# Reordering the second product of a fused attention kernel and shifting its operands by 64 bytes

One core of one Trainium2 chip. The metric is the device time of one execution in microseconds (us), the slowest core's, as the median of several runs. All runs quoted were at full TensorE clock (granted 0.998 or 0.999) unless a line says more.

## The reference

Attention over the 4,096 positions of four images, 128 channels for q and k, 256 for v, then a residual sum (biases and all but the layer's core left out):

```
q = x Wq + bq;  k = x Wk + bk;  v = x Wv + bv          # x: (4, 64, 64, 256)
energy    = einsum('bcn,bcm->bnm', pq, pk)             # pq, pk: (4, 128, 4096)
attention = softmax(energy, axis=-1)
out       = einsum('bcm,bnm->bcn', pv, attention)      # pv: (4, 256, 4096)
return gamma * out.reshape(x.shape) + x
```

## The kernel before

The kernel works on 16 groups of 256 columns n per image, and in each on eight steps t of 512 rows m. It gets float32 accuracy out of TensorE's float32r by splitting operands: p = exp(energy) goes to h (rounded down), l and d (combinations of the rest), v to vh, vl and vd. A step has three parts on TensorE: twelve matmuls of energies for a step three ahead (weights k, moving rows q), and the second product of its own step, 24 matmuls: h with vh, l with vl, d with vd, for two blocks j of n and four blocks i of m. In each, a slice of h, l or d is the weights, and a row of v (258 or 256 numbers per partition) moves.

```python
xpool, xtpool, qkv = pool("xpool", 3), pool("xtpool", 3), pool("qkv", 1)
ppool, work, kpool = pool("ppool", 2), pool("work", 2), pool("kpool", 3)
...
vh = qkv.tile([P, NM, VC], F32R, tag="vh", name="vh")     # NM = 32 rows, VC = C + 4 = 260
vl = qkv.tile([P, NM, VC], F32R, tag="vl", name="vl")     # columns C, C+1 are ones: the sums
vd = qkv.tile([P, NM, C], F32R, tag="vd", name="vd")
...
def energy(b, u, k):
    ...
    for i in range(2):
        for to, f, first, last in ((sa, 0, True, False), (sa, 1, False, True), (sb, 2, True, True)):
            nc.tensor.matmul(
                to[:, i], kt[:, 2 * k + i, f, :], q[:, :, f, :], start=first, stop=last
            )
...
def attend(b, u, j):
    ...
    for out_, left, right in ((a, h, vh), (a, l, vl), (bb[:, j, :], d, vd)):
        for i in range(4):
            m = 2 * t + i // 2 + NI * (i % 2)
            nc.tensor.matmul(
                out_, left[:, i, n], right[:, m, : out_.shape[1]],
                start=..., stop=..., skip_group_check=True,
            )
...
for k in range(2):
    if ahead < STEPS:
        energy(b, ahead, k)
    ...
for j in range(NJ):
    attend(b, u, j)
```

Tiles lie one behind another in SBUF in the order in which their pools are made: x's, then vh, vl, vd, then ppool (x, y, h, l, d), work (q among others), kpool (k).

## Time and profile before

| | before |
|---|---|
| time, median (range) of the runs beside the changed kernel | 2500.35 us (2498.88 to 2501.34) |
| PE busy / weight loads busy | 99% / 98% |
| VectorE / ScalarE busy | 84% / 72% |

How to read what follows: matmuls overlap in the trace and their ends are modelled, so I use **start-to-start times**: from one matmul's start to the next one's. Their sum is the time of TensorE's stream. In a timeline line, the first number is the start of the first of the merged instructions, so the difference of two lines' starts divided by the count is the mean start-to-start time. The lines of before that matter are shown in the prediction.

### The profile page before, as it was taken

What the parts mean: (1) busy time and instruction counts of PE and PEld (TensorE: products, weight loads), DVE (VectorE), ACT (ScalarE), POOL (GpSimd) and SP (SyncE); (2) the same over time, 40 slices, a digit from 0 to 9 for tenths busy, and PEclk for the clock granted to TensorE, in tenths of its full rate; (3) what the DMA queues carried; (4) which work ended last, traced back from release to release, by engine and by line L of the source; (5) the groups of instructions that cost most, each with busy time, mean ns of one, the idle gap of its engine ahead of it and who ended that gap; (6) DMA issues with size and microseconds to landing.
All of it is one profiled execution on the core that took longest, in us unless ns stands there. A gap on an engine that the chain in (4) does not pass through costs nothing.

```text
span 2497.3 us, 50025 instructions
## 1 busy us (share of the span) xinstructions
PE 2483.7 (99%) x19982; PEld 2442.8 (98%) x19982; DVE 2103.2 (84%) x2440; ACT 1807.1 (72%) x3138; POOL 425.7 (17%) x780
## 2 busy tenths in 40 slices
PE   9999999999999999999999999999999999999998
PEld 8999999999899999999989999999998999999998
DVE  5888888888698888888869888888886988888887
ACT  5777777776677777777667777777766777777775
POOL 4211111111411111111041111111114111111110
PEclk9999999999999999999999999999999999999999
DMA  7766666664766666666477666666648666666663
GB/s 240 219 193 208 202 207 195 193 209 148 242 214 196 202 202 208 200 194 204 138 245 220 202 190 207 206 202 197 192 144 255 212 203 198 196 208 203 200 194 106
DMA packets 137408, 498.92 MB, mean 200 GB/s; under 512 B 15536, under 2 KB 57264, under 8 KB 137168
## 3 DMA queue, kind: packets, MB, share of 16 engines
q0 software_dynamic: 92320, 453.17, 58.2%
q1 hardware_dynamic: 44304, 42.22, 5.6%
q8 instruction: 160, 2.62, 0.4%
q14 instruction: 80, 0.66, 0.1%
q10 hardware_dynamic: 544, 0.26, 0.0%
HBM read 445.25 MB, written 50.33 MB: 198 GB/s over the span
## 4 chain that ended last, share of the span: by engine, by line
PE 97%; ACT 2%; DVE 1%; issue 0%; DMA 0%; SPq 0%; ACTq 0%; DVEq 0%
PE a L364 38%; PE bb L364 19%; PE sa L316 19%; PE sb L316 10%; PE qk L136 4%; PE v L157 4%; PE ot L410 1%; PE xt L123 1%; ACT h L335 1%; DVE x L330 1%; ACT x L320 0%; ACT y L320 0%; DVE vd L283 0%; DMA x<-in_x_dram 0%; ACT vh L280 0%
## 5 line engine op out<-in xcount | busy, mean ns | idle before, releaser
L320 ACT ACTIVATE x<-sa 128x512 f32<-128x512 f32 x1024 | 608.8, 595 | 409.2 <-PE sa L316 329.6
L330 DVE TENSOR_TENSOR x<-x,y 128x1024 f32<-128x1024 f32 x512 | 625.8, 1222 | 159.2 <-ACT y L320 159.2
L316 PE MATMUL sa<-q,k 128*128 128x256 f32 x4096 | 749.9, 281 | 0.3
L364 PE MATMUL a<-vh,h 128*128 128x258 f32 x4096 | 661.2, 283 | 0.0
L364 PE MATMUL a<-vl,l 128*128 128x258 f32 x4096 | 658.2, 283 | 0.0
L364 PE MATMUL bb<-vd,d 128*128 128x256 f32 x4096 | 654.3, 282 | 0.0
L316 PEld LDWEIGHTS sa<-q,k 128*128 128x128 f32 x4096 | 625.7, 189 | 1.7 <-ACT x L320 1.1
L344 DVE SCALAR_TENSOR_TENSOR d<-h,x 128x1024 fp32r<-128x1024 f32 x512 | 624.2, 1219 | 0.0
L341 DVE TENSOR_TENSOR l<-x,h 128x1024 fp32r<-128x1024 f32 x512 | 624.1, 1219 | 0.0
L320 ACT ACTIVATE y<-sb 128x512 f32<-128x512 f32 x1024 | 612.8, 598 | 0.0
L316 PE MATMUL sb<-q,k 128*128 128x256 f32 x2048 | 578.6, 283 | 0.0
L335 ACT ACTIVATE h<-x 128x1024 fp32r<-128x1024 f32 x512 | 543.7, 1062 | 38.5 <-DVE x L330 37.7
L364 PEld LDWEIGHTS a<-vl,l 128*128 128x128 f32 x4096 | 563.6, 190 | 0.0
L364 PEld LDWEIGHTS bb<-vd,d 128*128 128x128 f32 x4096 | 560.6, 189 | 0.0
L364 PEld LDWEIGHTS a<-vh,h 128*128 128x128 f32 x4096 | 559.1, 189 | 0.0
L300 POOL DMA_DIRECT2D k<-kf x512 | 280.4, 548 | 1488.9 <-PE sb L316 1466.5
L316 PEld LDWEIGHTS sb<-q,k 128*128 128x128 f32 x2048 | 384.4, 188 | 8.1 <-ACT y L320 0.8
L136 PE MATMUL qk<-wqk_sb,xts 128*128 128x256 f32 x512 | 121.3, 380 | 0.0
L157 PE MATMUL v<-xts,wv_sb 128*128 128x256 f32 x512 | 120.3, 379 | 0.0
L157 PEld LDWEIGHTS v<-xts,wv_sb 128*128 128x128 f32 x512 | 97.3, 190 | 13.2
L402 ACT ACTIVATE o<-o,r 128x256 f32<-128x256 f32 x126 | 57.5, 504 | 72.5 <-DVE r L385 72.5
L136 PEld LDWEIGHTS qk<-wqk_sb,xts 128*128 128x128 f32 x512 | 92.3, 190 | 10.4 <-ACT xts L129 0.5
(54 smaller groups left out, 883.5 us busy)
## 6 DMA issues: line engine op xcount, KB each, us to landing
k<-kf POOLq DMA_DIRECT2D x512, 768.0 KB, 4.8
x<-in_x_dram SPq DMA_DIRECT2D x128, 256.0 KB, 3.7
kf<-f POOLq DMA_DIRECT2D x64, 384.0 KB, 4.0
out_dram<-x POOLq DMA_DIRECT2D x63, 256.0 KB, 2.5
qd<-qks POOLq DMA_DIRECT2D x128, 64.0 KB, 2.9
qr<-qd SPq DMA_DIRECT2D x64, 128.0 KB, 3.0
wv_sb<-in_L_conv_Wv_dram POOLq DMA_DIRECT2D x1, 256.0 KB, 5.7
out_dram<-x SPq DMA_DIRECT2D x1, 256.0 KB, 4.0
```

The lines of the kernel that those rows point to most:

```text
L123: nc.tensor.transpose(tp[:, k, s, :], self.xs[i][:, s, k * P : (k + 1) * P], ident,)
L136: nc.tensor.matmul(qk[:, s, :], self.xt[i][:, k, s, :], wqk_sb[:, k, :], start=(k == 0), stop=(k == KC - 1),)
L157: nc.tensor.matmul(vp[:, eh, :], wv_sb[:, k, eh * P : (eh + 1) * P], self.xt[i][:, k].rearrange("p s a -> p (s a)"), start=(k == 0), stop= ...
L300: nc.gpsimd.dma_start(t.rearrange("p (i s) f d -> p i s (f d)", s=2), kf[b, u % NU])
L316: nc.tensor.matmul(to[:, i], kt[:, 2 * k + i, f, :], q[:, :, f, :], start=first, stop=last)
L320: nc.scalar.activation(to[:, 2 * k : 2 * k + 2, :], sp.rearrange("p i j d -> p i (j d)"), AF.Exp, scale=scale,)
L330: nc.vector.tensor_tensor(x, x, y, ALU.mult)
L335: nc.scalar.activation(h, units[b, u], AF.Identity, scale=UPPER)
L341: nc.vector.tensor_tensor(l, x, h.bitcast(F32), ALU.subtract)
L344: nc.vector.scalar_tensor_tensor(d, h.bitcast(F32), 1.0 + E, x, ALU.mult, ALU.subtract)
L364: nc.tensor.matmul(out_, left[:, i, n], right[:, m, : out_.shape[1]], start=(t == i == 0 and (left is h or left is d and j == 0)), stop=(t ...
L402: nc.scalar.activation(o[:, j, :], o[:, j, :], AF.Identity, scale=r[:, j : j + 1])
```

## The change

Its intent: the same matmuls in another order and place. All of h's products, then all of l's, then all of d's, so that d's eight run into the twelve energies; and a pad of 64 bytes behind v, which shifts everything that follows. Cut to its core:

```diff
         xpool, xtpool, qkv = pool("xpool", 3), pool("xtpool", 3), pool("qkv", 1)
+        pool("pad", 1).tile([P, 16], F32, name="pad")
         ppool, work, kpool = pool("ppool", 2), pool("work", 2), pool("kpool", 3)
@@
-        def attend(b, u, j):
+        def attend(b, u):
@@
-            for out_, left, right in ((a, h, vh), (a, l, vl), (bb[:, j, :], d, vd)):
-                for i in range(4):
-                    m = 2 * t + i // 2 + NI * (i % 2)
-                    nc.tensor.matmul(out_, left[:, i, n], right[:, m, : out_.shape[1]], ...)
+            for left, right in ((h, vh), (l, vl), (d, vd)):
+                for j in range(NJ):
+                    out_ = bb[:, j, :] if left is d else acc[j]
+                    for i in range(4):
+                        m = 2 * t + i // 2 + NI * (i % 2)
+                        nc.tensor.matmul(out_, left[:, i, j * P : (j + 1) * P], right[:, m, : out_.shape[1]], ...)
@@
-                for j in range(NJ):
-                    attend(b, u, j)
+                attend(b, u)
```

More of the change, by code (lines that the diff above doesn't have):

```diff
@@ L347, in halves @@
             units[b, u] = h, l, d
-        def attend(b, u, j):
+        def attend(b, u):
             g, t = divmod(u, NU)
-            if t == j == 0:
+            if t == 0:
                 now["acc"] = [
@@ L357, in attend @@
             h, l, d = units[b, u]
-            a, bb = now["acc"][j], now["bb"]
-            n = slice(j * P, (j + 1) * P)
-            for out_, left, right in ((a, h, vh), (a, l, vl), (bb[:, j, :], d, vd)):
-                for i in range(4):
-                    m = 2 * t + i // 2 + NI * (i % 2)
-                    nc.tensor.matmul(
-                        out_,
-                        left[:, i, n],
-                        right[:, m, : out_.shape[1]],
-                        start=(t == i == 0 and (left is h or left is d and j == 0)),
-                        stop=(t == NU - 1 and i == 3 and left is not h),
-                        skip_group_check=True,
-                    )
-            if t == NU - 1 and j == NJ - 1 and (b, g) != (B - 1, NG - 1):
+            acc, bb = now["acc"], now["bb"]
+            for left, right in ((h, vh), (l, vl), (d, vd)):
[3 more added lines that the diff above has]
+                        m = 2 * t + i // 2 + NI * (i % 2)
+                        nc.tensor.matmul(
+                            out_,
+                            left[:, i, j * P : (j + 1) * P],
+                            right[:, m, : out_.shape[1]],
+                            start=(t == i == 0 and (left is h or left is d and j == 0)),
+                            stop=(t == NU - 1 and i == 3 and left is not h),
+                            skip_group_check=True,
+                        )
+            if t == NU - 1 and (b, g) != (B - 1, NG - 1):
                 now["o"] = work.tile([P, NJ, C], F32, tag="o", name=f"o_{b}_{g}")
```

## The prediction

> **What bounds the kernel now.** I read the page first: the busy table and the chain that ended last.
>
> ```profile
> PE 2483.7 (99%) x19982; PEld 2442.8 (98%) x19982; DVE 2103.2 (84%) x2440; ACT 1807.1 (72%) x3138; POOL 425.7 (17%) x780
> PEclk9999999999999999999999999999999999999999
> PE 97%; ACT 2%; DVE 1%; issue 0%; DMA 0%; SPq 0%; ACTq 0%; DVEq 0%
> PE a L364 38%; PE bb L364 19%; PE sa L316 19%; PE sb L316 10%; PE qk L136 4%; PE v L157 4%; PE ot L410 1%; PE xt L123 1%; ACT h L335 1%; DVE x L330 1%; ACT x L320 0%; ACT y L320 0%; DVE vd L283 0%; DMA x<-in_x_dram 0%; ACT vh L280 0%
> ```
>
> TensorE is the end of the kernel: 97% of the chain, at full clock, and its weight loads are busy for 98% of the span. 57% of the chain are the second product's matmuls (L364: a from h and l, bb from d), 29% the energies (L316). Nobody can take work from the path here; the only thing to win is the pace of one matmul after another. So next I read the waits of PE, and then its timeline.
>
> ```profile
> PE wp L197 <- POOL ident masks.py:199: 2.4, 1, 2.4
> PE ot L451 <- DVE o L446: 1.5, 1, 1.5
> PE xt L123 <- DMA x<-in_x_dram: 1.0, 1, 1.0
> ```
>
> The matmuls' own waits in the whole span are these 5 us. Now the timeline of PE in a quiet stretch (columns: start us, length us, engine, line, operation, operands, count). The lengths overlap and are modelled; the starts are what I use.
>
> ```profile
> 404.06 0.40 PE L316 MATMUL sa<-q,k 128*128 128x256 f32 x2
> ...
> 405.48 0.64 PE L364 MATMUL a<-vh,h 128*128 128x258 f32 x4
> 405.96 0.65 PE L364 MATMUL a<-vl,l 128*128 128x258 f32 x4
> 406.44 0.64 PE L364 MATMUL bb<-vd,d 128*128 128x256 f32 x4
> 406.92 0.64 PE L364 MATMUL a<-vh,h 128*128 128x258 f32 x4
> 407.40 0.65 PE L364 MATMUL a<-vl,l 128*128 128x258 f32 x4
> 407.88 0.64 PE L364 MATMUL bb<-vd,d 128*128 128x256 f32 x4
> 408.37 0.39 PE L316 MATMUL sa<-q,k 128*128 128x256 f32 x2
> ...
> 409.73 0.65 PE L364 MATMUL a<-vh,h 128*128 128x258 f32 x4
> ```
>
> The reader is to see two things. The twelve energies that start at 404.06 take until 405.48, 1.42 us or 118 ns each; the twelve that start at 408.37 take 1.36 us, 113 ns each. They are the same instructions on the same shapes with the same operands' spacing. And the second product takes 0.47 to 0.49 us for four, 118 to 122 ns each, whether its moving rows are 258 or 256 wide.
>
> I then took the start-to-start time of every matmul from the trace, leaving out those over 160 ns. Means: h 120.0 ns, l 120.0, d 119.1 (4096 of each), energies 116.2 (6144). I also sorted the energy blocks by their pace. Of 436 undisturbed blocks of twelve, 174 (40%) run at 113.3 ns throughout, but for at most the first, and 262 (60%) at 117.8 ns throughout. I call these **locked** and **unlocked**. No undisturbed unlocked block becomes locked midway. Which it will be is fixed by the step: with t the step of eight within a group, the energies after t = 4, 5 and 6 are nearly always locked, those after t = 1, 2, 3 and 7 unlocked (t = 0 has the output transposes in between). The pattern repeats from group to group to the nanosecond, so it comes from operands' addresses and timing and not from what other engines happen to do. Sorting d's matmuls by the ScalarE or VectorE operation beside them moves their mean by under 2 ns, with no sign that any one of these writes is the cause.
>
> **Where the change's 64 bytes come in.** From the code, per partition: d's tile lies 73,728 bytes behind vd's (vd itself 32,768, then ten tiles of 4,096), a multiple of 1,024, and rows and slices of both step in multiples of 512. So d's weights and the moving vd rows begin at the same place modulo 512: distance 0. k lies 16,448 bytes behind q, 64 over a multiple of 1,024, and steps in multiples of 512: distance 64. Distance 64 is the pair that can lock; distance 0 never stays at 113 ns in this trace. vh and vl have rows of 1,040 bytes, so their distance to h and l walks by 16 bytes from row to row and passes through every value.
>
> **What the Trainium skill says.** "TensorE: Matmul & The Clock Gate", LDWEIGHTS (loading the stationary operand): 128 columns take 128/1.2 = 107 ns. Back-to-back issue gap, same page: 256 moving columns at full clock take 256/2.4 + 2.5 = 109 ns. So loading and multiplying are balanced; the trace's best is 113.3 ns, a little above both, and the mean of the second product is 7 ns above that. The page "SBUF — State Buffer", Who interferes with whom, gives TensorE two independent read ports (moving rows and weights) and says that it never waits on anyone. The trace does not bear that out fully: two paces for the same energies. "Perfetto Trace Analysis", Identifying the Most-Contended Engine, tells to judge TensorE by the busy share of weight loads: 98%, which agrees with a path made of load, matmul, load. No page states a rule on the distance of weights and moving rows.
>
> **The change part by part.** It removes nothing and adds no instruction on TensorE: 12,288 matmuls of the second product before and after.
>
> 1. *The pad.* All tiles after v's shift by 64 bytes. q and k shift together, so the energies keep distance 64. d gets distance 64 from vd, exactly the energies'. h and l move by 64 against vh and vl. That is a step of four rows, two steps of t; since t runs through all values, the same set of distances occurs, only at other t. So I expect no change of the mean for h and l, 120.0 ns.
>
> 2. *The order.* Before, a step is E(12) h l d h l d with four of each; after, E(12) h(8) l(8) d(8). So each d block runs into the next energies, and the eight d's and twelve energies become one run of 20 with one distance. If the state is kept through a run, as it is in the energies now, all 20 are at 113.3 or all at 117.8 ns. The switch from one form to another has no cost of its own in the trace (h to l 120.8 ns beside 120.9 inside h), so having fewer switches saves nothing as such.
>
> 3. *How often a run locks.* The entry is now from l's last product. I can't read its phase out of a trace of before, so I take the share at which energies lock now on coming from another distance: 40%, or 3 of 7 values of t. Blocks that were broken by the transposes lock somewhat more often. I choose 45%. Pace: 0.45 x 113.3 + 0.55 x 117.8 = 115.8 ns.
>
> 4. *Sum.* d: (119.1 - 115.8) x 4,096 = 13.5 us saved. Energies: (116.2 - 115.8) x 6,144 = 2.5 us saved. Together 16 us. All of it is on TensorE, thus on the path. 2501 - 16 = 2485 us.
>
> 5. *Beside the path.* At a group's end the sums of a0 and a1 are now whole some 1 us earlier, but the kernel waits for bb's copy by ScalarE before VectorE frees a0 and a1; bb ends at the same place. In the group change that I looked at, a1 is free at 422.66 us. Its next use comes 4 matmuls after a0's at 422.50 instead of 12, at about 423.04: 0.4 us to spare. The first h of a group already loses 56 ns (a semaphore instruction of 51 ns in the weight queue): 63 x 56 ns = 3.5 us; a second one for a1 would cost 3 us, which I count in the range. l and d are needed later within a step than before, so VectorE (84% busy) gains slack.
>
> **The rivals.** (a) *All runs lock*, as the change's wording hopes: d and energies at 113.3, (119.1 - 113.3) x 4,096 + (116.2 - 113.3) x 6,144 = 24 + 18 = 42 us, 2459 us. For it: one distance throughout, and a locked block stays locked. Against it: 60% of the energy blocks don't lock today with that very distance, and the entry still comes from l, whose distance walks. (b) *None lock*: d 117.8 saves 5 us, the energies lose 1.6 x 6,144 = 10 us: 2506 us. For it: the new entry could miss at every t, since the outcome is fixed by t and not random; against it: eight values of t, of which 3 of 7 hit now. (c) *h and l move too*: runs of eight at one form could meet better or worse phases. Their times spread by some 3 ns over the steps' positions; over about 60 to 130 different positions the mean is good to 0.3 to 0.4 ns, that is 3 us of their 8,192. (d) *A wait takes the gain*: in the energies after the output transposes two or three intervals of about 200 ns wait for ScalarE to free their buffers; there a faster TensorE only waits longer. That is 60 of 512 blocks, some 10% of the energies' part.
>
> **Range and chances.** Step 3 is nearly all of the uncertainty. With eight values of t locking at 45%, the share has a spread of 0.18, times 4.5 ns x 10,240 = 8 us; with (c) and the semaphore some 10 us. The change was evidently made by someone who saw the energies' pace, so I lean a little to the faster side: 2483 us, range 2464 to 2498. Faster by over 2% needs under 2451 us, beyond even rival (a), and so h and l faster by over 1 ns each as well: 4%. Slower by over 2% (2551 us) has no mechanism but a new wait: 1%. Within 2%: 95%.
>
> **What would show it.** d's mean start-to-start time falls to 114 to 118 ns and takes the same two values as the energies; in the timeline a d block of eight (about 0.91 or 0.94 us) and the energies after it have one pace. h and l stay within 0.5 ns of 120.0. The share of locked energy blocks says where in the range the time falls. PE's waits stay at some 5 us, clock and counts unchanged. It is wrong if d and the energies after it don't share a pace, if d stays at 119 ns, if h or l move by over 1 ns, or if a wait for a1 or bb appears at the group changes.

## The result

2494.33 us (2493.11 to 2495.51, four runs) against 2500.35: ratio 0.9976, 95% interval 0.9959 to 0.9994. A ratio is the mean time of one kernel's fast runs over that of the other's of the same rounds, so not quite the ratio of the medians quoted. The time lies within my range, but the gain is 6 us where I had forecast 18.

The page of the changed kernel, busy times and chain:

```profile
PE 2478.3 (99%) x19982; PEld 2436.0 (98%) x19982; DVE 2108.0 (85%) x2440; ACT 1808.3 (73%) x3138; POOL 425.0 (17%) x780
PEclk9999999999999999999999999999999999999999
PE 97%; ACT 2%; DVE 1%; issue 0%; DMA 0%; SPq 0%; ACTq 0%; DVEq 0%
```

The bound is the same: TensorE, full clock, the same 19,982 matmuls. Its waits, from the waits of PE, have not grown either:

```profile
PE wp L197 <- POOL ident masks.py:199: 2.4, 1, 2.4
PE xt L123 <- DMA x<-in_x_dram: 1.2, 1, 1.2
PE ot L455 <- DVE o L450: 1.1, 1, 1.1
PE sa L318 <- ACT x L322: 0.7, 4, 0.2
```

So again everything is in the pace. Sums of start-to-start times in the two traces, in us, with the mean in ns of those from 100 to 160 ns, and, for the energies, the share of undisturbed blocks of twelve that I count as locked. Undisturbed means that no start-to-start time in the block is over 160 ns; locked, that the mean of its first eleven is under 115.5 ns:

| | before: sum, mean | after: sum, mean | difference |
|---|---|---|---|
| h (4,096) | 495.0, 120.0 | 493.2, 119.6 | -1.8 |
| l (4,096) | 491.5, 120.0 | 491.1, 119.9 | -0.4 |
| d (4,096) | 489.1, 119.0 | 478.4, 116.5 | -10.7 |
| energies (6,144) | 736.1, 116.1 | 743.3, 117.0 | +7.2 |
| all else | 274.7 | 275.0 | +0.4 |
| locked energy blocks | 174 of 432 (40%) | 64 of 432 (15%) | |

Two thirds of what d gained went back in the energies. The count of locked blocks hides a difference in kind: in before, 172 of the 174 are at 113 ns from the second matmul on; in the changed kernel none of the 64 is. They start at 118 ns, behind d's that were unlocked, and come down to 113 at the fifth matmul. The timeline of PE in the changed kernel shows how (start us, length us, engine, line, operation, operands, count):

```profile
411.22 1.07 PE L368 MATMUL bb<-vd,d 128*128 128x256 f32 x8
412.13 0.40 PE L318 MATMUL sa<-q,k 128*128 128x256 f32 x2
...
413.54 1.13 PE L368 MATMUL a<-vh,h 128*128 128x258 f32 x8
414.50 1.12 PE L368 MATMUL a<-vl,l 128*128 128x258 f32 x8
415.46 1.10 PE L368 MATMUL bb<-vd,d 128*128 128x256 f32 x8
```

The eight d's take 0.91 us, 113.8 ns each: they have locked. The twelve energies right behind them take 1.41 us, 117.5 ns each: they have not. In the trace, 243 undisturbed energy blocks follow a d that was locked (its fifth to seventh times under 115 ns), and not one of them is locked.

### The profile page after: what moved, and what is told of

It is laid out like the page before. It is cut to its first block, busy times and chain, and to the rows that moved or that the text cites. A ratio compares the mean times of both kernels' runs of the same rounds, so it can differ in the third digit from the quotient of the medians.

```text
span 2492.0 us, 50085 instructions
## 1 busy us (share of the span) xinstructions
PE 2478.3 (99%) x19982; PEld 2436.0 (98%) x19982; DVE 2108.0 (85%) x2440; ACT 1808.3 (73%) x3138; POOL 425.0 (17%) x780
## 4 chain that ended last, share of the span: by engine, by line
PE 97%; ACT 2%; DVE 1%; issue 0%; DMA 0%; SPq 0%; ACTq 0%; DVEq 0%
PE a L368 38%; PE sa L318 19%; PE bb L368 19%; PE sb L318 10%; PE qk L136 4%; PE v L157 4%; PE ot L414 1%; PE xt L123 1%; ACT h L337 1%; DVE x L332 1%; ACT x L322 0%; ACT y L322 0%; DMA x<-in_x_dram 0%; DVE vd L285 0%; ACT vh L282 0%
## 5 line engine op out<-in xcount | busy, mean ns | idle before, releaser
L368 PE MATMUL a<-vh,h 128*128 128x258 f32 x4096 | 576.6, 283 | 0.0
L368 PE MATMUL a<-vl,l 128*128 128x258 f32 x4096 | 574.2, 283 | 0.0
L368 PE MATMUL bb<-vd,d 128*128 128x256 f32 x4096 | 559.9, 279 | 0.0
L368 PEld LDWEIGHTS a<-vl,l 128*128 128x128 f32 x4096 | 526.9, 190 | 0.0
L368 PEld LDWEIGHTS a<-vh,h 128*128 128x128 f32 x4096 | 524.0, 189 | 0.0
L368 PEld LDWEIGHTS bb<-vd,d 128*128 128x128 f32 x4096 | 515.1, 189 | 0.0
L398 DVE SCALAR_TENSOR_TENSOR o<-a,o 128x256 f32<-128x256 f32 x126 | 47.5, 419 | 87.2 <-ACT o L378 87.2
```

The costliest lines, as they stand in the source:

```text
L368: nc.tensor.matmul(out_, left[:, i, j * P : (j + 1) * P], right[:, m, : out_.shape[1]], start=(t == i == 0 and (left is h or left is d and ...
L398: nc.vector.scalar_tensor_tensor(o[:, j, :], a[:, :C], 1.0 + E, o[:, j, :], ALU.mult, ALU.add)
```

## The experiments

First, what I had overlooked. I call *distance* the place of the weights that are loaded beside a matmul less the place of its moving rows, within a partition, modulo 512. Weights are loaded one matmul ahead (in before, the load for the h that starts at 401.21 us starts at 401.10, just behind the start of the last energy at 401.09), so at the boundary the pair is vd's row and **k**. The pad shifts k as well as d. So k, which had stood 64 behind vd's places, now stands 128 behind; and q, which had stood at vd's own places (modulo 512), stands 64 behind. The run of 20 "with one distance" that I had predicted has 64 seven times, 128 once, 64 again, and its moving rows change place in between.

My theory for the experiments: the distance of each pair sets the pace, a settled state is carried on only if nothing changes at the boundary. The rivals: the order itself brought d's gain; or the switch from d's to the energies' operands unlocks whatever the places.

Places modulo 512, behind vd's row, in the kernels compared, worked out from the tiles' sizes and order in the code (the traces hold no addresses):

| | order | h, l, d | q | k | d's pairs | boundary | energies' pairs |
|---|---|---|---|---|---|---|---|
| before | old | 0 | 0 | 64 | 0 | 64 | 64 |
| after | new | 64 | 64 | 128 | 64 | 128 | 64 |
| order alone | new | 0 | 0 | 64 | 0 | 64 | 64 |
| pad alone | old | 64 | 64 | 128 | 64 | 128 | 64 |
| one distance | new | 64 | 0 | 64 | 64 | 64 | 64 |
| two pads | new | 64 | 128 | 192 | 64 | 192 | 64 |

### The order alone

The changed kernel without the line `pool("pad", 1).tile([P, 16], F32, name="pad")`.

> The new order alone, without the pad: d's weights at distance 0 from vd's rows, k at 64 from both q and vd. Theory (the distance between a matmul's moving rows and the weights that are loaded beside it sets the pace; order alone is neutral): d stays at 118.5 to 119.5 ns, h and l at 120 within 0.6 ns, and 2493 to 2505 us, with the share of locked energy blocks the only thing that moves it. Rival 1 (the order itself, runs of eight of one form, brought d's gain): d at 116.8 ns as after, energies no worse, under 2492 us.

Measured: 2510.37 us (before on the same chip 2501.45, ratio 1.0035, 1.0021 to 1.0048): **slower than before** by 0.35%, and 5 us over my upper end. d 118.8 ns and h and l 120.4 and 119.9, as expected; but not one of 432 undisturbed energy blocks is locked, and the energies went to 117.9 ns. Rival 1 falls: the order alone gives d nothing. And the share of locked blocks, 40% before, isn't a property of the energies but of how each step enters them.

### The pad alone

```diff
+        pool("pad", 1).tile([P, 16], F32, name="pad")
         ppool, work, kpool = pool("ppool", 2), pool("work", 2), pool("kpool", 3)
```

> The pad alone, in the old order: d at 64 from vd, but k now at 128 from vd (64 from q). Theory: d's fours lock in part, d 116 to 118 ns; the last d before the energies loads k at distance 128, stalls (118 ns or more), and the energies are locked in under 25% of undisturbed blocks, mean 116.8 or more; 2492 to 2502 us. Rival 1 (order is what helps d): d at 119 ns, energies 40% locked as before, 2500 us.

Measured: 2498.94 us (ratio 0.9989, 0.9983 to 0.9996). d 117.7 ns and the last d 119.1 as expected. But 184 of 431 energy blocks (43%) are locked where I had expected under 25%, and the energies' mean is 116.2 ns, under my 116.8. None of the 184 is locked from its start: they begin at 117 to 118 ns and come down to 113 at the fifth or sixth matmul. So a stalled boundary doesn't keep energies from settling later; why some steps do and others don't is not shown.

### One distance

```diff
-        pool("pad", 1).tile([P, 16], F32, name="pad")
-        ppool, work, kpool = pool("ppool", 2), pool("work", 2), pool("kpool", 3)
+        work, kpool, ppool = pool("work", 2), pool("kpool", 3), pool("ppool", 2)
```

work and kpool together take 45,120 bytes, 64 over a multiple of 1,024, so h, l and d come to 64 behind v's places with no pad, while q and k stay where they were.

> The new order, no pad; the tiles of q and k are placed ahead of those of h, l and d. So q stands at 0, k at 64 and h, l, d at 64 from v's rows: every matmul from the first d to the last energy has one distance, the boundary from d to k too. Theory (the boundary at distance 128 cost the lock): d as after, 116 to 117 ns, the last d no slower than the others, and blocks that are locked at d's end stay so: at least 45% of undisturbed energy blocks locked, energies at 115.9 ns or less, 2478 to 2489 us, faster than both kernels. Rival 2 (the switch from d's to the energies' operands unlocks, whatever the distance): last d at 118 or more, energies under 25% locked, 2491 to 2498 us.

Measured: **2483.06 us** (2482.59 to 2484.97), ratio to before 0.9926, 0.9912 to 0.9939. Its interval lies wholly below the changed kernel's, so it beats both. d 116.0 ns, energies 115.1, 305 of 432 blocks locked (71%). In the timeline d and the energies now share a pace, 0.93 us for eight with the entry, and 1.36 us for twelve (113.3 ns each), twice in a row:

```profile
407.70 1.09 PE L367 MATMUL bb<-vd,d 128*128 128x256 f32 x8
408.63 0.39 PE L317 MATMUL sa<-q,k 128*128 128x256 f32 x2
...
409.99 1.12 PE L367 MATMUL a<-vh,h 128*128 128x258 f32 x8
410.95 1.11 PE L367 MATMUL a<-vl,l 128*128 128x258 f32 x8
411.90 1.09 PE L367 MATMUL bb<-vd,d 128*128 128x256 f32 x8
412.83 0.39 PE L317 MATMUL sa<-q,k 128*128 128x256 f32 x2
...
414.19 1.14 PE L367 MATMUL a<-vh,h 128*128 128x258 f32 x8
```

And the carrying-over is without exception: 305 blocks after a locked d are all locked, from the first matmul on, and 127 after an unlocked d are all unlocked. Rival 2 falls.

### Two pads

```diff
-        ppool, work, kpool = pool("ppool", 2), pool("work", 2), pool("kpool", 3)
+        ppool = pool("ppool", 2)
+        pool("pad2", 1).tile([P, 16], F32, name="pad2")
+        work, kpool = pool("work", 2), pool("kpool", 3)
```

> The changed kernel with a second pad of 64 bytes between d's pool and q's and k's: h, l, d at 64, q at 128, k at 192 from vd. So d and the energies keep 64 each, and the boundary has 192, which is 64 modulo 128. If the distance counts modulo 128: as with one distance, at least 45% of energy blocks locked, 2478 to 2490 us. If it counts modulo 256 or more: the boundary still stalls (118 ns or more), under 25% locked, 2491 to 2498 us.

Measured: 2496.55 us (ratio 0.9979, 0.9970 to 0.9988), with 66 of 432 blocks locked (15%). All 66 come behind an unlocked d and settle midway; of 363 blocks behind a locked d none locks. The time fits the second reading, but the reason is neither of the two. Start-to-start times in ns for step t = 5 (the eight d's, then the first six energies; means over the groups):

```
order alone   119.3 119.4 116.6 118.3 119.2 120.7 116.9 117.4 | 117.6 118.3 117.5 117.6 118.3 117.5
after         113.1 113.7 113.5 113.4 113.5 113.4 113.4 117.6 | 114.2 118.3 117.6 117.5 118.4 117.4
two pads      123.0 116.7 116.0 114.3 113.5 113.7 113.5 113.8 | 116.8 119.0 117.5 118.3 117.4 117.3
one distance  120.9 114.1 123.5 118.3 113.2 113.6 113.4 113.2 | 113.6 113.4 113.2 113.6 113.4 113.2
```

With two pads the boundary matmul (the eighth) doesn't stall, 113.8 ns against 117.6 in the changed kernel: 192 is as good as 64 there. Yet the first energy takes 116.8 and the lock is gone. What else differs from the kernel with one distance is where the energies' pair lies: q is 128 behind vd, and k, 64 further, 192. A look at when locked matmuls start says why that matters. 113.33 ns is 17 times 6.67 ns, and within one trace the starts of locked matmuls of one kind all leave the same remainder modulo 6.67 ns (apart from a slow drift). Between the energies and the d's of the same 100 us, that remainder differs by 0.0 ns (6.65 of 6.67) in the kernel with one distance, by 1.7 ns in the changed kernel (q's rows 64 further) and by 3.3 ns with two pads (128 further). So in these traces a lock belongs to a point in time that goes with where the pair of rows and weights lies, and d's lock is the energies' lock only where the two pairs' places agree. Rows and weights shift together in all of these kernels, so whether the rows' place or the weights' sets that point is not separated. The time spans of the boundaries in the table come from the same traces; the cause inside the chip is not shown by them.

### The old order on the good placement

The kernel before with the pools in the order work, kpool, ppool, and nothing else.

> The placement with one distance (q at 0; k, h, l, d at 64 from v's rows), in the OLD order (fours). Theory (a lock needs several matmuls at distance 64 to settle and is carried on where distance and rows' place stay): a four of d before h is too short to lock often, the four before the energies carries whatever it has reached: d 117 to 118.5 ns, where d's last is locked the energies are too, no energy block locked after an unlocked d and the reverse; 2484 to 2498 us, so the order is worth 2 to 14 us on this placement. Rival (the placement alone is all): d and energies as in the run with both, 2481 to 2485 us.

Measured: 2489.43 us (ratio 0.9954, 0.9940 to 0.9967). d 118.0 ns, energies 114.5, 368 of 432 blocks locked (85%). So the placement is worth 11 us in the old order, and the new order 6 us more on it (2489.4 to 2483.1, on two chips; 7 us by the ratios to before), while without the placement the new order costs 9 us (2501.5 to 2510.4). The gain of the order is d's (118.0 to 116.0 ns), since a four is often still settling when h comes; the energies even lock in fewer steps than with fours. My expectation that energies lock only behind a locked d missed as I had worded it: none of the fours of d runs at 113 ns throughout, and yet 368 blocks behind them are locked. In six of the eight steps (t = 0, 2 and 4 to 7) the four (of d's matmuls) is still settling when it hands over, and the energies behind it are at 113 ns from the first or the second on, at the same distance.

### Why h and l stay slow: fixed rows

h and l have 8,192 matmuls at 120 ns. Four kernels with a wrong result on purpose ask why. Their edit on the kernel with one distance, for row 0:

```diff
-                            right[:, m, : out_.shape[1]],
+                            right[:, m if right is vd else 0, : out_.shape[1]],
```

> Wrong result on purpose: the kernel with one distance in the new order, but h's and l's products always take row 0 of vh and vl (258 wide as before), so that they too have distance 64 with the rows at one place, and the whole step of 36 has one distance. Theory (h and l are slow because their rows walk by 16 bytes and never settle): nearly everything at 113.3 to 114 ns, h and l under 115; 2405 to 2435 us. Rival (h and l are slow for their 258 columns or because they add up in two banks): h and l stay at 118 ns or more, 2465 us or more.

Measured: 2480.27 us (ratio 0.9919). d 114.9 and energies 114.0 (426 of 432 blocks locked), since every step now enters d in the same way; but h and l at 120.4 and 120.8 ns. **My theory for h and l falls**: at a constant distance of 64 they keep a pattern of eight times from 118 to 125 ns and never settle at 113.

> Wrong result on purpose: as the run with row 0, but always row 4 of vh and vl, which lies 64 bytes further modulo 128, so that h and l have distance 0 throughout (d and the energies keep 64). Theory: h and l settle at some 120 ns (distance 0 keeps one pace of 120), no block of them at 113; 2465 to 2500 us. Rival (any fixed row is fast, for instance because it is read again and again): under 115 ns.

Measured (one look, state unknown): 2492.86 us; h and l 120.1 and 120.4 ns. The mean is as expected for distance 0, but the one pace isn't: after the first few matmuls five of the eight steps stay at 120 ns, and the steps t = 2, 4 and 6 have a pattern of 114 to 125. The row 0 run makes the mean less telling, too.

> Wrong result on purpose: as before, always row 2 of vh and vl, 32 bytes into a 64: distance 32 for h and l. Theory says only that they settle at one pace; I expect it between 115 and 121 ns, not at 113.3, and thus 2440 to 2490 us. If 113.3 shows here too, then distance 64 isn't special and only distance 0 is bad.

Measured (one look): 2474.94 us; h and l 120.2 and 120.0 ns. Within what I expected, and no faster than distance 64.

All three have 258 columns. The next takes the width away (h's and l's outputs `acc[j][:, :C]`; the sums are set to 1 from the accumulator with one operation of the same form on VectorE):

> Wrong result on purpose: as the run with row 0, but h and l take 256 columns in place of 258 (the sums are set to 1). If the width of 258 is what keeps h and l from settling at distance 64: h and l at 113.3 to 114.5 ns, nearly the whole step at one pace, 2405 to 2430 us. If it is something else of h and l (two accumulators in two banks, both forms on one row): they stay at 118 ns or more, 2465 to 2480 us.

Measured (one look, state unknown): **2423.88 us**, before on the same chip 2502.74. h and l 113.6 ns, d 113.6, energies 114.2. The timeline of this kernel shows the whole step at one pace, 0.90 to 0.91 us for each eight, 1.37 us for the twelve, 113 to 114 ns per matmul:

```profile
407.58 1.07 PE L367 MATMUL a<-vh,h 128*128 128x256 f32 x8
408.49 1.07 PE L367 MATMUL a<-vl,l 128*128 128x256 f32 x8
409.39 1.07 PE L367 MATMUL bb<-vd,d 128*128 128x256 f32 x8
410.30 0.39 PE L317 MATMUL sa<-q,k 128*128 128x256 f32 x2
...
411.67 1.13 PE L367 MATMUL a<-vh,h 128*128 128x256 f32 x8
```

Beside it the same stretch of the run with row 0 and 258 columns, in which h and l take 0.96 to 0.97 us:

```profile
408.88 1.12 PE L367 MATMUL a<-vh,h 128*128 128x258 f32 x8
409.85 1.13 PE L367 MATMUL a<-vl,l 128*128 128x258 f32 x8
410.81 1.08 PE L367 MATMUL bb<-vd,d 128*128 128x256 f32 x8
411.73 0.39 PE L317 MATMUL sa<-q,k 128*128 128x256 f32 x2
```

So two columns out of 258 cost 7 ns in each of 8,192 matmuls here, with rows at one place, and not 1 part in 129.

> Wrong result on purpose: the kernel with one distance and its own walking rows (1,040 bytes apart), h and l 256 wide, sums set to 1. If the width alone counts: h and l near 114 ns and 2405 to 2435 us. If the walk by 16 bytes alone is enough to keep them slow: h and l at 118 to 121 ns and 2470 to 2490 us. I expect the second: both the width and the walk stand in the way.

Measured (one look): 2469.35 us; h and l 118.2 and 118.0 ns, near the low end of what I expected (and the time just under it). So of the widths tried only 256 reached 113 ns, and it is not enough: with rows that walk by 16 bytes it is worth 1.5 to 2 ns, with rows at one place 7.

> Wrong result on purpose: as the run with row 0, but 264 columns for h and l (row 0 and the first four elements of row 1; the sums stay right). 264 is a multiple of 8 and 258 isn't. If a width that is a multiple of 8 is what a lock needs: h and l in one steady pace, 113 to 117 ns, 2405 to 2445 us. If any width over 256 is too long to lock: 118 ns or more, 2470 to 2495 us.

Measured (one look): 2492.78 us; h 123.3 ns, l 120.2, the l's at 120 throughout. A multiple of 8 isn't what counts; what I can say is that 258 and 264 don't reach 113 at a distance of 64 and 256 does.

A kernel with a right result in this form would need v's rows 1,024 bytes apart and the softmax sums from elsewhere. I found no cheap place for these (four more matmuls per step for the sums would, as an estimate from the times above, cost 4 x 113 ns for 16 x 6.5 saved), so that version is left open.

### Another entry

The kernel with one distance, forms in the order l, h, d (and the start and stop flags of the accumulation moved from h to l).

> The placement with one distance, the forms in the order l, h, d: the entry to d now comes from h, the same rows otherwise. Theory (which steps lock is decided anew by where the entry falls, d's state is carried into the energies in every undisturbed block): no energy block differs from d's state, but other steps lock than with h, l, d, and 3 to 8 of 8 steps do: 2474 to 2496 us. Rival (this placement locks most steps whatever comes before): the same steps, some 70% locked, 2481 to 2485 us.

Measured: 2484.72 us (ratio 0.9937, 0.9923 to 0.9950), beside 0.9926 for the order h, l, d: no difference. 306 of 432 blocks locked, after the same steps t as before. The rival was right. The entry comes from a form of the same width whose rows walk in the same way, so swapping h and l may change nothing that d sees; that is argued, not tested. As before, every block of energies has d's state.

## Why the prediction was right and where it was wrong

- **The bound, and what can change.** Right: TensorE, its pace alone, no new wait. The second semaphore that I feared came (the trace has 123 instead of 63 in the weight queue of this line), but h still has just 63 times over 160 ns, of 10.9 us together against 11.0. One reading was loose: the "120.9 inside h" includes these 63 stalls; without them it is 119.7, so the switch from h to l did cost some 1 ns. It changes nothing in the sum.
- **Step 1, the pad.** Right for d (64 from vd) and for h and l (119.6 and 119.9 ns, expected 120.0). It named the energies' own distance rightly, too. It didn't ask for the pair at the boundary.
- **Step 2, the order: the step that failed.** "The eight d's and twelve energies become one run of 20 with one distance" is not so. The pad moves k too, so the pair at the boundary has 128, and the moving rows change place by 64. 243 times of 243 a locked d was followed by unlocked energies (363 of 363 with two pads). Where the places agree (one distance) the state is carried over 305 times of 305, as step 2 had it. That an unlocked block never locks midway held in before, but not in the changed kernel: its 64 locked blocks did just that.
- **Step 3, the share.** I took 45% for d and energies alike, from 40% seen before. The energies had 15%. Over the correct kernels the share was 0, 15, 15, 40, 43, 71, 71 and 85%: it goes with how the eight steps of each kernel enter, and one kernel's share says next to nothing on another's. My spread of 0.18 fitted independent chances, but the mean that I put it around was not known.
- **Step 4, the sum.** d: 13.5 us predicted, 10.7 measured. Energies: 2.5 saved predicted, 7.2 lost. h and l: 0 predicted, 2.2 saved. That is 16 us against 5.7 in the two traces, or 5.3 with all else. (The sum started from 119.1 and 116.2 ns; I get 119.0 and 116.1 from the same trace, which would have made it 15 us.) The energies' term is the one that was mis-signed; with the places put right it comes out (one distance: d 12.7 us, energies 3.0 us saved from the same sums).
- **The rivals.** None of them was this one. I had (a) all lock, (b) none lock, each for d and energies together; what happened is that d mostly locks and the energies mostly don't. What I had said would show me wrong, "if d and the energies after it don't share a pace", is what the first timeline showed.

What stays open: whether the boundary's 128 alone would have been enough to lose the lock (two pads shows that it is also lost without a stall at the boundary, with q and k 128 further on); whether q's place or k's does it, since the two always moved together; why some unlocked blocks settle midway; and by what in the chip a distance or a place sets the pace.

## What to carry to other kernels

When TensorE alternates weight loads and matmuls of equal length, look at start-to-start times by kind and by position before looking for waits: one shape with two exact paces was here the sign that the places of operands in SBUF matter. A shift for one pair shifts every tile behind it, so write down the places for all pairs, and above all for those where one loop hands over to the next; a reordering of pools can give the wanted places without a pad. Judge order and placement together, since here the same new order cost 9 us on one placement and won 6 on another, and don't forecast a share of lucky entries from another kernel's share.

## What the Trainium skill lacked or had wrong

- "TensorE: Matmul & The Clock Gate", Back-to-back issue gap, has for a stream of load and matmul pairs only two figures, about 81 ns at 128 columns and 131 at 512; its formula by columns, from which the prediction took 109 ns, it calls that of an isolated matmul. In these runs pairs of load and matmul with 256 columns took 113.3 ns (17 x 6.67) when settled, 117.8 ns in the unlocked energies, and 119.0 on average in d before; a shift of tiles changed that at the same shapes. The page has nothing on the places of weights and moving rows. By that formula 258 columns would be an estimated 2/2.4 = 0.8 ns above 256; in the runs on row 0 h and l took 120.4 and 120.8 ns with 258 columns and 113.6 with 256.
- "SBUF — State Buffer", Who interferes with whom, has TensorE's two read ports independent and TensorE waiting on nobody. The pace here went with the distance between what the two read: moving h, l and d by 64 behind v's rows, with q and k where they were, took d from 118.8 ns (order alone) to 116.0 (one distance), in the same order.
- No page has that a settled stream keeps its starts at a fixed remainder of 6.67 ns, or that a pair of rows and weights placed 64 or 128 bytes further settles 1.7 or 3.3 ns later within that remainder.
